# Sparse graph attention, one core: packed biases, planned constants, three more x buffers, norm constants by two tiles, and a new order of all work

## The chip, the cores and the metric

The kernel runs on one core of one Trainium2 chip. The metric is device time in microseconds (us) of one execution. Each number beside "time" is a median over runs; the profile comes from one execution.

## The reference, cut to what matters

x has 16 batches of 1024 rows with 512 columns; adj is one 1024 x 1024 matrix of zeros and ones, shared by all batches. Everything is float32.

```
h = jnp.maximum(_layernorm(x, axis=-1), 0.0)
q = (h @ Wq + bq).reshape(b, n, H, HD)        # H = 8, HD = 64; k and v likewise
scores = jnp.einsum('bihd,bjhd->bhij', q, k) / jnp.sqrt(jnp.float32(HD))
scores = scores + jnp.where(adj == 0, -1e9, 0.0)[None, None, :, :]
weights = jax.nn.softmax(scores, axis=-1)
out = jnp.einsum('bhij,bjhd->bihd', weights, v)
x = x + out.reshape(b, n, H * HD)
```

adj has few ones: most rows have a handful of neighbours, a few have many. So the kernel computes only the scores of neighbours.

## The kernel before, in words

**Once, at the start.** The kernel counts each row's neighbours (`degree`), ranks the rows by that count (`rank_of`, `ranks`), and from then on handles the rows in ranked order, in 8 tiles of 128 rows. Tile 0 has the rows with most neighbours. `CAPS` gives how many neighbour places each tile has (11, 8, 6, 5, 4, 3, 3, 2); what the rows of tile 0 have beyond is cut into pieces of 4 that get a pseudo tile, -1. The tables of neighbours are built by VectorE and scattered and collected through DRAM by DMAs (`list_of`, `spread`, `tell`, `collect`, `spots`); the chain `longest`, `count_pieces`, `first_piece`, `owners`, `pieces`, `slots` makes the places of the pieces. `first_piece` (line 794, `p_before`) is a matmul in it, and so stands in TensorE's queue.

**Each batch.** For each tile n: `load_x` (line 609, an indirect DMA from GpSimd's queue), `stats` on VectorE (L618, L619), then for a group of four tiles together `variance` on VectorE (L627), `power` on GpSimd (L630) and `shift` on VectorE (L634), then `norm` on ScalarE (L644), `flip` (four transposes on TensorE, L651), `unflip` (ScalarE copies to hT, L656), `proj_kv` (two projections on TensorE, one bias matmul L659 and four matmuls L661 each; each float32 matmul shows as two passes in the trace), `evict_kv` (ScalarE, L672), `store_kv` (an SP DMA into a key and value table in DRAM). When all 8 tiles of a batch are stored, rows of this table can be gathered. Batch 0's keys and values are made in a first pass over the rows in their given order (n = -8 to -1, names with `first`), while the ranks are still being found.

The attention goes by units. A unit is a tile with 2, 3 or 4 of its neighbour places; a batch has 14 units. For each: `queries` (a projection, L661 with `pq`), `gather` (GpSimd issues one indirect DMA of 512 KB for each place, L885; a row's own place comes by SP), `multiply` (VectorE, L895, which frees the query's PSUM buffer), `score` (L899), `exponent` (ScalarE, L903), for the tiles 4 to 7 `share`, then the weighing of v: one place on VectorE in some units (`weigh_v`, L915), the others on ScalarE (`weigh_s`, 8 activations a place, L921), `fold` (L926, on VectorE, or on GpSimd for the units in `POOL_FOLDS`) and `join` (L932) or `add_up` (TensorE, L944), `scale` (L976), `residual` (L985) and `put_out` (L988, an indirect DMA from GpSimd). An x tile is held from its load to its `put_out`.

**Buffers.** `POOLS` names how many buffers each pool has: 14 for x, 11 for hT, 2 for queries in PSUM, 2 for keys and values in PSUM, 2 for flips, 6 for gathered units.

**What sets the order.** Nothing is scheduled at run time. Each engine runs its own queue in order. The order is made when the program is built: `plan_of` (line 172) adds every operation to a `Plan` with its engine, a planned length and delay, what it follows, the buffers it uses, and a *place*, a number that ranks it. `Plan.ordered` (line 97) plays these through: whenever an engine is free in this planned time, it takes the ready operation with the lowest place. The list that results is the order in which the instructions are written. The last batch's units come in `LAST_ORDER`, tile 0 first.

**Biases.** Each bias is split into three bf16 parts that add up to it, in three rows of its own tile: `round` (ScalarE cast, L520), `remain` (GpSimd subtraction, L524), three times for each of k, v, q. The bias matmul uses `chosen`, which is one in these three rows:

```
def load_b(name):
    for start in starts:
        nc.sync.dma_start(rest[name][start : start + 1, :], vectors[name].rearrange("(o n) -> o n", o=1))
def round(name, j):
    rows = slice(starts[j], P)
    nc.scalar.copy(bias[name][rows, :], rest[name][rows, :])
```

Memsets and iotas for constants are issued at the very start of GpSimd's queue, ahead of all planned work.

**At the end.** `sums` (128 x 128 x 8) holds all row sums; `all_rows_fine` (line 1111) reduces it twice over 1024 elements (L1117, L1118), and a branch at the end reads the verdict.

Of the kernel before, what the change touches and what calls it, by code (L numbers as in the profile page):

```python
# [46 lines left out]
UNITS = (  # L47
    (7, 0, 2),
    (6, 0, 3),
    (5, 0, 3),  # L50
    (4, 0, 4),
    (3, 0, 3),
    (3, 3, 2),
    (2, 0, 3),
    (2, 3, 3),
    (1, 0, 4),
    (1, 4, 4),
    (0, 0, 4),
    (-1, 0, 4),
    (0, 4, 4),  # L60
    (0, 8, 3),
)
SHARES = (7, 6, 5, 4)
DIRECT = (7, 6, 5, 4, 3, 2, 1)
LAST_ORDER = (10, 11, 12, 13, 8, 9, 6, 7, 4, 5, 3, 2, 1, 0)
LAST_DIRECT = (7,)
POOL_FOLDS = (2, 3, 8, 9, 11)
# [5 lines left out]
ONE_MORE = (6,)  # L73
BY_VECTOR_LAST = {2: 1, 3: 1, 4: 1}
VECTOR_RESIDUAL = (4,)
POOLS = dict(x=14, h=2, pht=2, hT=11, pkv=2, kvt=3, q=2, q0=1, g=6, acc=2, o=1)


class Plan:
# [8 lines left out]
    def __init__(self):  # L88
        self.ops = []
        self.number = {}  # L90

    def add(self, key, engine, length, place, after=(), uses=(), delay=0.15, moves=0.0):

        self.number[key] = len(self.ops)
        self.ops.append((key, engine, length, place, after, uses, delay, moves))

    def ordered(self, bufs):
        ops = self.ops
# [29 lines left out]
        free = dict.fromkeys(engines, 0.0)  # L128
        moved = now = 0.0
        events = []  # L130
        result = []
        while True:
            for e in engines:
# [3 lines left out]
                while ready[e]:  # L137
                    place, i = heapq.heappop(ready[e])
                    key, _, length, _, _, uses, delay, moves = ops[i]
                    if can_start(ops[i]):  # L140
                        for use in uses:
                            if use not in has:
                                has.add(use)
                                given[use[0]] += 1
                        result.append(key)
                        free[e] = end = now + length
                        heapq.heappush(events, (end, -1))
                        if moves:
                            end = moved = max(moved, end) + moves
                        heapq.heappush(events, (end + delay, i))  # L150
                        break
# [16 lines left out]
        assert len(result) == len(ops)  # L168
        return result


def plan_of(B):

    plan = Plan()
    add = plan.add
    tiles, units, rate = B * NT, B * NU, NU / NT

    names = "kvq"
    sources = ("g", -3)
    first = range(-NT, 0)  # L180

# [4 lines left out]
    size = dict(load_x=0.75, load_w=3.0, load_adj=1.5, load_b=0.0)  # L186
    add(("zeros",), "SP", 0.15, -70, delay=2.0)
    for k, load in enumerate(loads):
        uses = [("x", load[1])] if load[0] == "load_x" else []
        add(load, "SP", 0.9 if load[0] == "load_b" else 0.2, -90 + k, uses=uses, delay=4.6, moves=size[load[0]])  # L190
    for j in range(3):
        for k, name in enumerate(names):
            place = -70 + 4 * k + j
            add(("round", name, j), "ACT", 0.58, place, [("remain", name, j - 1) if j else ("load_b", name)])
            if j < 2:
                add(("remain", name, j), "POOL", 1.3, place, [("round", name, j)])
    for t in range(NT):
        add(("degree", t), "DVE", 1.5, -60 + t, [("load_adj", t)])
        add(("no_diagonal", t), "POOL", 0.3, -60 + t, [("degree", t)])
    add(("keys",), "DVE", 0.4, -50, [("degree", t) for t in range(NT)], [sources])  # L200
    for what, known, made in (("key", [("keys",)], -48.59), ("rank", [("ranks",)], -37.92)):
        for half in range(2):
            row = ("q", what, half)
            add(("flip_row", what, half), "PE", 0.6, made, known, [row])
            add(("copy_row", what, half), ("DVE", "ACT")[half], 0.65, made, [("flip_row", what, half)], [row, sources])
    rows = lambda what: [("copy_row", what, half) for half in range(2)]
    for t in range(NT):
        add(("rank_of", t), ("DVE", "ACT")[t >= NT // 2], 1.25, (-53.17, -45.38)[t >= NT // 2], rows("key"))
    add(("ranks",), "DVE", 1.4, -47, [("rank_of", t) for t in range(NT)])
    add(("ends",), "DVE", 0.7, -45, rows("rank"), [sources])  # L210
    for t in range(NT):
        add(("list_of", t), "DVE", 2.5, -32.19 + t, [("ends",), ("no_diagonal", t)], [sources])
        behind = lambda name: [(name, t - 2)] if t > 1 else [("zeros",)]
        add(("tell", t), "POOL", 1.3, -38.67 + 0.3 * t, [("ranks",), ("shift", (t - NT) // 2)] + behind("tell"), delay=2.0)
        add(("spread", t), "POOL", 1.3, -45.82 + t, [("list_of", t)] + behind("spread"), delay=2.0)
    add(("collect", "told"), "SP", 0.05, -39, [("tell", t) for t in range(NT)], delay=2.6)
    add(("collect", "lists"), "SP", 0.05, -31, [("spread", t) for t in range(NT)], delay=2.6)
    add(("others",), "DVE", 1.3, -16.12, [("ends",)], [sources])
    add(("perm_of",), "DVE", 0.5, -31, [("collect", "told")])
    add(("spots",), "DVE", 3.9, -38.36, [("collect", "lists")])  # L220
    add(("long_rows",), "POOL", 1.3, -26.80, [("perm_of",)], [("g", -2)], 2.5, 1.5)
    add(("long_blocks", 0), "DVE", 1.25, -18.02, [("long_rows",), ("others",)], [sources, ("g", -2)])
    for k in range(1, 5):
        add(("long_blocks", k), "DVE", 2.0, -41.10 + 0.1 * k, [("long_blocks", k - 1)], [("g", -2)])
    for k in range(1, ROUNDS):
        known = [("long_blocks", 4), ("spots",)] if k == 1 else [("longest", k - 1)]
        add(("longest", k), "DVE", 1.1 if k == 1 else 0.8, --0.41 + 0.5 * k, known, [("g", -2)])
    a, own, lists = (("acc", "pieces", k) for k in range(3))
    add(("count_pieces",), "DVE", 0.9, 7.23, [("longest", ROUNDS - 1)])
    add(("first_piece",), "PE", 0.3, 2.20, [("count_pieces",)], [a])  # L230
    add(("owners",), "DVE", 0.9, 2.21, [("first_piece",)], [a])
    add(("flip_owners",), "PE", 0.3, 2.22, [("owners",)], [own])
    add(("copy_owners",), "DVE", 0.25, 2.23, [("flip_owners",)], [own])
    add(("list_pieces",), "PE", 0.4, 2.24, [("owners",)], [lists])
    add(("pieces",), "DVE", 1.1, 2.25, [("list_pieces",)], [lists])
    add(("slots", 0), "DVE", 2.0, 2.24, [("pieces",), ("spots",)])

    for n in range(-NT, tiles):
        b, j = divmod(n, NT)
        ahead = 0 if n >= 0 else 60 if n < 4 - NT else 19.47 - 1.3 * j  # L240
        p = (b - 1) * NU + j * rate if b > 0 else j * rate - 20.77 if b == 0 else 1.5 * j - 42.92
        if n >= 0:
            known = [("perm_of",)] if b == 0 else []
            add(("load_x", n), "POOL", 1.35, p - 5.47, known, [("x", n)], delay=4.5, moves=0.75)
        if b:
            add(("stats", n), "DVE", 0.84, p - ahead - 4.00, [("load_x", n)], [("x", n)])
        m, k, size = group_of(n)
        if b and k == size - 1:
            add(("variance", m), "DVE", 0.33, p - ahead - 5.38, [("stats", n - k) for k in range(size)])
            add(("power", m), "POOL", 1.1, p - ahead - 4.87, [("variance", m)])  # L250
            add(("shift", m), "DVE", 0.37, p - ahead - 4.29, [("power", m)])
        add(("norm", n), "ACT", 0.76, p - 6.38, [("shift", m) if b else ("load_x", n)], [("x", n), ("h", n)], delay=0.00)
        add(("flip", n), "PE", 0.62, p - 3.43, [("norm", n)], [("h", n), ("pht", n)])
        add(("unflip", n), "ACT", 0.53, p - 2.57, [("flip", n)], [("pht", n), ("hT", n)])
        if b == 0:
            continue
        for w in range(2):
            e = p - -0.51 + 0.3 * w + (1.41 if n < 3 - NT and w else 0.0)
            ready = [("unflip", n)]
            if n < 0:  # L260
                ready += [("round", "kv"[w], 2), ("load_w", "kv"[w])]
            add(("proj_kv", n, w), "PE", 3.70, e, ready, [("hT", n), ("pkv", n, w)])
            add(("evict_kv", n, w), "ACT", 0.53, e - 0.99, [("proj_kv", n, w)], [("pkv", n, w), ("kvt", n)])
        ready = [("evict_kv", n, w) for w in range(2)]
        if n >= 0:
            add(("store_kv", n), "SP", 0.1, p, ready, [("kvt", n)], delay=2.5, moves=1.5)
        else:
            add(("store_kv", n), "POOL", 1.35, p, ready + [("ranks",)] + ([("store_kv", n - 1)] if n > -NT else []), [("kvt", n)], delay=2.5, moves=1.5)

    q_of = {}  # L270
    one_by_one = []
    for k in range(units):
# [3 lines left out]
        i = b * NU + (LAST_ORDER.index(u) if b == B - 1 else u)  # L276
        t, _, count = UNITS[u]
        n = b * NT + NT - 1 - t
        q = ("q", b, t)
        if q not in q_of:  # L280
            p = i - 2.12
            if t >= 0:
                ready = [("unflip", n)] + ([("round", "q", 2), ("load_w", "q")] if b == 0 else [])
                add(("queries", b, t), "PE", 3.66, p, ready, [("hT", n), q])
                if t == 0:
                    add(("copy_q", b), "ACT", 0.57, p + 0.5, [("queries", b, 0)], [q, ("q0", b)])
            else:
                add(("queries", b, t), "PE", 0.9, p, [("copy_q", b)], [q, ("q0", b)])
# [4 lines left out]
        for s, slot in enumerate(slots):  # L293
            if is_own(u, s):
                add(slot, "SP", 0.1, i - -0.48, stored if b == 0 else [("store_kv", n)], [g], delay=2.5, moves=1.5)
                continue
            add(slot, "POOL", 1.35, i - 1.86 + 0.1 * s, stored, [g], delay=4.0, moves=1.5)
        vector = by_vector(b, B, u)
        add(("multiply", k), "DVE", 0.1 + 0.533 * count, i, slots + [q_of[q]], [g, q])
        add(("score", k), "DVE", 0.1 + 0.533 * count, i - -0.03, [("multiply", k)], [g])  # L300
# [887 lines left out]
```

## Time and profile before

| what | value |
|---|---|
| time, three runs | 1720.81 us median (1717.02 to 1721.78) |
| span of the profiled execution | 1721.4 us; the page gives no other time for this execution |
| instructions | 19566 |
| eight passes of one projection at full clock (L661 x8) | 3.60 us |
| bytes moved by DMA | 531.73 MB, 309 GB/s on average |
| TensorE busy in a stretch of 40 us, eight stretches from 320 us on | 36.5 to 40.0 us |

In the profile a line gives the source line, engine, operation, output and inputs. In a timeline the first number is the start, the second the length, and brackets show how long the engine had been idle and what ended the wait. "issue" is time in which the engine waited for nothing that the profile shows.

### The profile page before, as it was taken

How to read it: one execution, taken by the hardware profiler on the slowest of the kernel's cores; microseconds unless marked ns; L12 is line 12 of the kernel's file. 1: busy time of each engine (PE TensorE's matmuls, PEld its weight loads, DVE VectorE, ACT ScalarE, POOL GpSimd, SP SyncE). 2: the span in 40 equal slices, each digit the busy share in tenths (PEclk: the TensorE clock that was granted, in tenths of full speed). 3: DMA queues.
4: the chain of work that ended last, by engine and by line, in shares of the span. 5: the costliest groups of instructions: out<-in, count | busy, mean ns of one | idle time of the engine just before them, and what ended most of it. 6: DMA issues, size and time to landing. Idle time of an engine off the chain costs nothing.

```text
span 1721.4 us, 19566 instructions
## 1 busy us (share of the span) xinstructions
PE 1601.7 (93%) x4295; PEld 740.1 (43%) x4295; DVE 1506.2 (87%) x1921; ACT 1479.7 (86%) x5484; POOL 1264.2 (73%) x1161
## 2 busy tenths in 40 slices
PE   6979999999999999999999999999999999999896
PEld 3434444444444444444444444444444444444332
DVE  6789889898989989899998889989888998988896
ACT  5249989898998989899898989989898997979895
POOL 4757777787877778777877778778687777867654
PEclk9989999999999999999999999999999999999998
DMA  6397889899898989989898898889989888988893
GB/s 235 122 319 269 313 309 348 315 336 331 305 327 303 360 309 331 325 306 326 306 358 320 308 338 301 324 311 338 337 317 329 298 318 312 336 329 290 299 356 141
DMA packets 150741, 531.73 MB, mean 309 GB/s; under 512 B 19916, under 2 KB 19916, under 8 KB 150616
## 3 DMA queue, kind: packets, MB, share of 16 engines
q0 software_dynamic: 109840, 390.70, 64.4%
q1 hardware_dynamic: 40776, 139.71, 21.4%
q8 instruction: 36, 0.59, 0.1%
q14 instruction: 89, 0.73, 0.1%
HBM read 429.51 MB, written 100.82 MB: 308 GB/s over the span
## 4 chain that ended last, share of the span: by engine, by line
PE 74%; DMA 9%; DVE 3%; POOL 2%; ACT 1%; issue 1%; DVEq 0%; POOLq 0%; ACTq 0%
PE pv L661 22%; PE pk L661 22%; PE pq L661 20%; DMA g<-kv,index 8%; PE acc L944 3%; DVE g L895 2%; PE pht L651 2%; PE pv L659 1%; PE pk L659 1%; PE pq L659 1%; POOL g L885 1%; DMA kv<-kvt 1%; ACT hT L656 0%; ACT h L644 0%; DMA out_dram<-x,perm 0%
## 5 line engine op out<-in xcount | busy, mean ns | idle before, releaser
L921 ACT ACTIVATE g<-g,weights 128x64 f32<-128x64 f32 x4696 | 1155.8, 338 | 15.1 <-DVE weights L908 14.3
L885 POOL DMA_INDIRECT g<-kv,index x608 | 631.3, 1038 | 225.7 <-issue 144.5
L895 DVE TENSOR_TENSOR g<-g,pq 128x1536 f32<-128x1536 f32 (+2 forms) x208 | 388.1, 1871 | 101.6 <-DMA g<-kv,index 73.7
L661 PE MATMUL pq<-wq,hT 128*128 128x512 f32 x1024 | 470.8, 603 | 0.0
L661 PE MATMUL pk<-wk,hT 128*128 128x512 f32 x960 | 431.5, 592 | 0.0
L661 PE MATMUL pv<-wv,hT 128*128 128x512 f32 x960 | 431.5, 592 | 0.0
L899 DVE TENSOR_REDUCE weights<-g 128x32 f32<-128x2048 f32 (+2 forms) x224 | 424.1, 1893 | 0.6
L661 PEld LDWEIGHTS pq<-wq,hT 128*128 128x128 f32 x1024 | 198.1, 193 | 273.9 <-issue 270.1
L926 DVE TENSOR_TENSOR g<-g 128x512 f32<-128x512 f32 (+1 forms) x301 | 257.7, 860 | 27.6 <-ACT g L921 27.2
L661 PEld LDWEIGHTS pv<-wv,hT 128*128 128x128 f32 x960 | 182.4, 190 | 215.1 <-issue 212.0
L661 PEld LDWEIGHTS pk<-wk,hT 128*128 128x128 f32 x960 | 182.4, 190 | 205.5 <-issue 202.0
L609 POOL DMA_INDIRECT x<-in_x_dram,perm x128 | 148.8, 1162 | 39.9 <-issue 33.6
L988 POOL DMA_INDIRECT out_dram<-x,perm x128 | 133.7, 1045 | 50.9 <-issue 19.9
L926 POOL TENSOR_TENSOR g<-g 128x512 f32<-128x512 f32 x90 | 118.9, 1321 | 67.5 <-DVE g L926 58.6
L915 DVE TENSOR_TENSOR g<-g,weights 128x512 f32<-128x512 f32 x149 | 124.3, 834 | 2.1 <-ACT weights L903 1.8
L644 ACT ACTIVATE h<-x,shift,rstd 128x512 f32<-128x512 f32 x120 | 94.5, 812 | 28.7 <-issue 14.7
L903 ACT ACTIVATE weights<-weights 128x32 f32<-128x32 f32 (+2 forms) x224 | 49.7, 222 | 71.9 <-DVE weights L899 71.8
L985 POOL TENSOR_TENSOR x<-x,o 128x512 f32<-128x512 f32 x67 | 89.3, 1333 | 11.5 <-DVE o L976 7.8
L944 PE MATMUL acc<-g,ident 128*128 128x512 f32 x170 | 86.4, 622 | 9.0 <-DMA g<-kv,index 5.4
L659 PE MATMUL pq<-bq_parts,chosen 128*128 128x512 bf16 x128 | 48.8, 382 | 47.9 <-DVE g L895 47.9
L651 PE MATMUL pht<-ident,h 128*128 128x128 f32 x512 | 73.8, 276 | 18.5 <-ACT hT L656 16.5
L651 PEld LDWEIGHTS pht<-ident,h 128*128 128x128 f32 x512 | 60.6, 142 | 64.7 <-issue 33.9
(231 smaller groups left out, 1147.5 us busy)
## 6 DMA issues: line engine op xcount, KB each, us to landing
g<-kv SPq DMA_DIRECT2D x128, 512.0 KB
kv<-kvt SPq DMA_DIRECT2D x120, 512.0 KB
g<-kv,index POOLq DMA_INDIRECT x608, 6.8
adj<-in_adj_dram SPq DMA_DIRECT2D x8, 512.0 KB
x_first<-in_x_dram SPq DMA_DIRECT2D x8, 256.0 KB
x<-in_x_dram,perm POOLq DMA_INDIRECT x128, 6.3
out_dram<-x,perm POOLq DMA_INDIRECT x128, 5.5
wk<-in_L_gnn_Wk_dram SPq DMA_DIRECT2D x1, 1024.0 KB
```

The source lines that it names most:

```text
L609: nc.gpsimd.indirect_dma_start(out=X[n][:], out_offset=None, in_=x_rows, in_offset=on(ap=perm[:, t : t + 1], axis=0), element_offset=b * N * D
L651: nc.tensor.transpose(PH[n][:, c, :], hn[:, ts(c, P)], ident)
L659: nc.tensor.matmul(pt, chosen, bias[name], start=True, stop=False)
L661: nc.tensor.matmul(pt, HT[n][:, c, :], W[name][:, c, :], start=False, stop=(c == DC - 1))
L885: nc.gpsimd.indirect_dma_start(out=G[i][:, s].rearrange("p j d -> p (j d)"), out_offset=None, in_=KV[b % len(KV)][:], in_offset=on(ap=inde ...
L895: nc.vector.tensor_tensor(k, k, Q[b, t][:, None, :].to_broadcast([P, count, D]), ALU.mult)
L899: nc.vector.tensor_reduce(weights[:, w, :], heads(G[i][:, :count, 0, :]), AX.X, ALU.add)
L915: nc.vector.tensor_tensor(v, v, own.to_broadcast([P, n, H, HD]), ALU.mult)
L921: nc.scalar.activation(v[:, h, :], v[:, h, :], AF.Identity, scale=weights[:, c + s, h : h + 1])
L926: engine.tensor_tensor(v[:, 0:n], v[:, 0:n], v[:, first : first + n], ALU.add)
L944: nc.tensor.matmul(ACC[b, home], owner_t if t < 0 else ident, v[:, s, :], start=(u == parts_of(home)[0] and s == 0), stop=(u == parts_of(h ...
L988: nc.gpsimd.indirect_dma_start(out=out_rows, out_offset=on(ap=perm[:, t : t + 1], axis=0), in_=X.pop(b * NT + NT - 1 - t)[:], in_offset=No ...
```

## The change

- The three biases share one tile: three copies of k's bias go to partitions 0 to 2, of v's to 32 to 34, of q's to 64 to 66, each by one DMA. `round` and `remain` handle all at once; which row keeps which part is set by a scale per partition (`parts_at` makes it from the identity). `chosen` has one block for each bias. The very first tile (n = -8) is projected without its bias, which a matmul of its own (`add_bias`) adds afterwards.
- Constants become planned operations (`setup`, three steps on GpSimd); two memsets move to VectorE; an activation on a constant, `warm`, stands first on ScalarE.
- x has 17 buffers instead of 14.
- `variance`, `power`, `shift` handle two tiles at a time instead of four.
- Row sums are kept for each batch; a new operation `seen` reduces them to a sum and a minimum per batch; the last check reduces 16 numbers of each.
- The plan's lengths and delays are new (`LENGTHS`, `PAIR`). The plan lets VectorE and GpSimd not run two operations of `SHARED` at the same planned time. All places are new (`AT`, and `FINE` for single operations), and the place of a unit grows by its share of the batch's slots instead of by one.
- `JOIN` is False, so `join_acc` is not used. `LAST_TILES` and `PARTS` give the units and their order as before; the units folded on GpSimd are the same.

Shortened diff:

```diff
-POOLS = dict(x=14, h=2, pht=2, hT=11, pkv=2, kvt=3, q=2, q0=1, g=6, acc=2, o=1)
+AT = dict(
+    load_x=106.07, stats=-2.83, variance=-3.87, power=-87.25, shift=-9.66, norm=-4.89, flip=-7.74, unflip=-31.23, proj_kv=-1.94,
+    evict_kv=38.12, queries=-1.19, own=55.32, gather=-1.08, score=6.6, exponent=29.51, row_sums=-147.93, share=2.3,
+    weigh_v=-2.68, weigh_s=90.78, fold=-2.21, join=-4.72, add_up=-1.79, direct_residual=35.08, direct_out=32.8, more=-13.17,
...
+POOLS = dict(x=17, h=2, pht=2, hT=11, pkv=2, kvt=3, q=2, q0=1, g=6, acc=2, o=1)
+GROUP = 2
+JOIN = False
...
+SHARED = ("fold", "join",  "weigh_v", "residual", "scale", "power")
...
+                    shared = e in port and key[0] in SHARED
+                    if can_start(ops[i]) and not (shared and port[other[e]] > now):
+                        if shared:
+                            port[e] = now + length
...
-            add(slot, "POOL", 1.35, i - 1.86 + 0.1 * s, stored, [g], delay=4.0, moves=1.5)
+            add(slot, "POOL", i + AT["gather"] + 0.1 * s, stored, [g])
...
-            add(("fold", k, *n), "POOL" if on_pool else "DVE", 1.4 if on_pool else 0.45 * n[1] + 0.35, i + 0.90, weighed, [g], delay=1.67 if on_pool else 0.15)
+            add(("fold", k, *n_), "POOL" if on_pool else "DVE", i + AT["fold"], weighed, [g], length=None if on_pool else PAIR[n_[1]])
...
-    size = 4 if n >= 0 else 2
+    size = GROUP if n >= 0 else 2
...
         def load_b(name):
-            for start in starts:
-                nc.sync.dma_start(rest[name][start : start + 1, :], vectors[name].rearrange("(o n) -> o n", o=1))
+            vec = vectors[name]
+            rows = bass.AP(tensor=vec.tensor, offset=vec.offset, ap=[[0, 3], [1, H * HD]])
+            g = names.index(name)
+            nc.sync.dma_start(rest[32 * g : 32 * g + 3, :], rows)
+
+        def warm():
+            nc.scalar.activation(warmed, minus_half, AF.Relu, bias=minus_half, scale=minus_half)
+
+        def parts_at():
+
+            ends_at = [once.tile([P, 1], F32, tag=f"ends{j}", name=f"ends_at_{j}") for j in range(2)]
+            for j in range(2):
+                nc.vector.tensor_reduce(ends_at[j], ident.rearrange("p (g r) -> p g r", r=32)[:, :, j], AX.X, ALU.add)
+            nc.vector.tensor_scalar(later[0], ends_at[0], -1.0, 1.0, op0=ALU.mult, op1=ALU.add)
+            nc.vector.tensor_tensor(later[1], later[0], ends_at[1], ALU.subtract)
+
+        def round(j):
+
+            if j < 2:
+                nc.scalar.activation(part, rest, AF.Identity, scale=later[j])
+            else:
+                nc.scalar.copy(bias, rest)
+
+        def remain(j):
+            nc.gpsimd.tensor_tensor(rest, rest, part, ALU.subtract)
...
+        def setup(k):
+
+            count_up = lambda to, base, step, by: nc.gpsimd.iota(
+                to, pattern=[[step, to.shape[-1]]], base=base, channel_multiplier=by, allow_small_or_imprecise_dtypes=True
+            )
+            if k == 0:
+                nc.gpsimd.memset(chosen, 0.0)
+                for g in range(len(names)):
+                    nc.gpsimd.memset(chosen[32 * g : 32 * g + 32, g, :], 1.0)
+            elif k == 1:
+                count_up(place, 0, P, 1)
+                nc.gpsimd.memset(before["lists"], 0.0)
+                nc.gpsimd.tensor_copy(before["told"][:, :, own], place)
+                count_up(limits, P, P, 0)
+            else:
+                count_up(small_iota, 0, 1, 0)
+                nc.gpsimd.memset(spot, 0.0)
+                nc.gpsimd.memset(weights, 0.0)
...
+        def add_bias(n, name):
+            pt = PT[n, names.index(name)]
+            nc.tensor.matmul(pt, chosen[:, names.index(name), :], bias, start=False, stop=True)
...
+        def seen(b):
+            nc.vector.tensor_reduce(sums[:, 0, b : b + 1], SUMS[b].rearrange("p t h -> p (t h)"), AX.X, ALU.add)
+            nc.vector.tensor_reduce(sums[:, 1, b : b + 1], SUMS.pop(b).rearrange("p t h -> p (t h)"), AX.X, ALU.min)
...
-    nc.vector.tensor_reduce(both[:, 0:1], flat, AX.X, ALU.add)
-    nc.vector.tensor_reduce(both[:, 1:2], flat, AX.X, ALU.min)
+    nc.vector.tensor_reduce(both[:, 0:1], sums[:, 0, :], AX.X, ALU.add)
+    nc.vector.tensor_reduce(both[:, 1:2], sums[:, 1, :], AX.X, ALU.min)
```

## The prediction, made before the changed kernel ran

> **What bounds the kernel now.** I read the page's busy table first, then a table of busy time by stage (start, first batch, the middle up to the last key and value projection, the rest), then TensorE's own rows in order of time, then the rows of the constants for the norm.
>
> ```profile
> PE 1601.7 (93%) x4295; PEld 740.1 (43%) x4295; DVE 1506.2 (87%) x1921; ACT 1479.7 (86%) x5484; POOL 1264.2 (73%) x1161
> ```
>
> ```profile
> 0.00:31.00 31.00, 13.87 (x44) 7.79 (x45) 18.28 (x51) 13.82 (x22) 16.80 (x37) 0.97 0.74 267
> 31.00:200.00 169.00, 155.69 (x442) 74.39 (x441) 145.85 (x290) 108.51 (x345) 113.78 (x105) 0.96 0.71 246
> 200.00:1616.00 1416.00, 1353.51 (x3636) 625.02 (x3635) 1262.09 (x1495) 1280.38 (x4799) 1074.41 (x962) 0.99 0.89 321
> 1616.00:1721.40 105.40, 78.66 (x176) 32.90 (x174) 79.93 (x88) 76.98 (x321) 59.21 (x57) 0.86 0.69 257
> ```
>
> Columns: stretch and length, then busy us of TensorE, its weight loads, VectorE, ScalarE and GpSimd, granted clock, DMA share, GB/s. TensorE's idle time is 17.1, 13.3, 62.4 and 26.7 us; it bounds the first three stages. The other engines and the DMAs are near it: in the middle VectorE is busy 89%, ScalarE 90%, DMA 89%.
>
> The middle is fourteen repeats of about 100.7 us (boundaries at 207, 308, ... 1618). One boundary, TensorE only:
>
> ```profile
> 307.88 1.02 PE L944 MATMUL acc<-g,owner_t 128*128 128x512 f32 x2
> 308.74 1.02 PE L944 MATMUL acc<-g,ident 128*128 128x512 f32 x2
> 311.64 0.38 PE L659 MATMUL pq<-bq_parts,chosen 128*128 128x512 bf16 x1 [1.88 <-DVE g L895]
> 311.86 3.59 PE L661 MATMUL pq<-wq,hT 128*128 128x512 f32 x8
> 315.29 1.02 PE L944 MATMUL acc<-g,ident 128*128 128x512 f32 x2
> 316.14 1.04 PE L651 MATMUL pht<-ident,h 128*128 128x128 f32 x8
> 318.44 0.38 PE L659 MATMUL pq<-bq_parts,chosen 128*128 128x512 bf16 x1 [1.26 <-DVE g L895]
> ```
>
> TensorE stops twice for a query buffer: the multiply that frees it waits for a gather, which waits for the last tile of the batch to be stored. No next-batch projection is at hand in between, for this reason:
>
> ```profile
> 305.08 0.64 DVE L618 BATCH_NORM_STATS2 st<-x 128x6 f32<-128x512 f32 x1
> 307.39 0.16 DVE L627 TENSOR_SCALAR rstd<-mv 128x4 f32<-128x4 f32 x1
> 312.04 1.53 POOL L630 TENSOR_TENSOR rstd<-rstd,minus_half 128x4 f32<-128x4 f32 x1
> 314.31 0.15 DVE L634 SCALAR_TENSOR_TENSOR shift<-mv,rstd 128x4 f32<-128x4 f32 x1
> 314.50 1.52 ACT L644 ACTIVATE h<-x,shift,rstd 128x512 f32<-128x512 f32 x2 [0.46 <-DVE shift L634]
> ```
>
> The constants wait until four tiles are loaded and measured, and the power then stands behind gathers on GpSimd. Loads of x at 293.84 wait for output of older tiles (1.86 us instead of 0.95). So the first new norm comes at 314.5, too late for the gap.
>
> The start and the end:
>
> ```profile
> 9.46 1.28 ACT L520 ACT_TABLE_LOAD   x1 [9.46 <-DMA scratch<-in_L_gnn_bk_dram]
> 11.51 1.15 POOL L524 TENSOR_TENSOR scratch<-scratch,bk_parts 64x512 f32<-64x512 f32 x1 [4.42 <-ACT bk_parts L520]
> 12.74 0.73 POOL L630 TENSOR_TENSOR before_told<-before_told,minus_half 128x2 f32<-128x2 f32 x1
> ...
> 1704.65 1.17 DVE L1117 TENSOR_REDUCE c_both<-sums 128x1 f32<-128x1024 f32 x1
> 1705.82 1.21 DVE L1118 TENSOR_REDUCE c_both<-sums 128x1 f32<-128x1024 f32 x1
> 1706.95 0.68 DVE L915 TENSOR_TENSOR g<-g,weights 128x512 f32<-128x512 f32 x1
> ```
>
> The first power, ready at 5.9, stands behind a bias subtraction that waits for a table load, which waits for a bias DMA. At the end two long reduces stand ahead of the last weighing.
>
> **The change, part by part, against the span of 1721.4 us.**
>
> Biases and the first operations. Nine casts (0.615 us, 5.5 on ScalarE) become three; six subtractions (1.155 us, 6.9 on GpSimd) two; nine 2 KB DMAs, which hold SP's queue from 2.6 to 10.2, three. Added are some four small VectorE operations (about 0.8 us, taking the 0.2 us of small rows). The power need no longer pass the bias chain: about 6.2 to 6.9, norm to 7.8, flip and copy to 9.2. The weights' landing is not shown: 1.5 MB at this stage's 267 GB/s plus the 3.1 us from the first load's issue (0.81) to its first use (3.92) gives about 9.5. So projections can begin at 9.5 instead of 17.25. Afterwards wv arrives behind 7 MB: about 29 us at that rate, as now (first pv at 29.79), so only the two further key projections of 3.65 us fit in earlier. I take idle time from 17.1 to 11: -6 (bounds -1 and -8).
>
> The index chain. TensorE's queue stands 8.40 us (to 105.1) behind p_before, placed too early in the order; VectorE makes its input at 104.8. With measured lengths in the plan work can be put ahead of it: -6 (bounds 0 and -8; if VectorE's chain were moved back for it, nothing).
>
> Middle. Constants by two and three more x buffers let two tiles be normed before the gap: one tile's pair of projections is 7.3 us, against gaps of 1.9 and 1.3. The fourteen boundaries hold 47.5 us of waiting for VectorE; a third flip in a row waits for ScalarE, 0.99 us fourteen times, and pairs of tiles avoid it. The other 1.0 are single waits. Of the 62.4 I leave 1.2 us per batch, 17: -45 (bounds: 0, if no tile is ready in time, to -60). After the gap the next limits are the gathers and VectorE: 89.8 us per batch against a new period near 97.
>
> The clock. After gaps of 1.37, 2.27, 4.11 and 3.74 us the eight passes behind them took 5.29, 5.29, 6.01 and 5.29 us instead of 3.60: 7.5 us together. The Trainium skill (TensorE: Matmul & The Clock Gate, HAM oscillation) asks only that idle gaps stay below about 3.4 us; by it the first two should be free and the gain at most 4.1. Here the row decides[...]. -5.
>
> Added work. Sixty powers instead of thirty: a two-column one took 0.714 us, a four-column one 1.206, so 42.8 instead of 36.2. Thirty more variances and shifts (0.16 each) are 9.5 us of VectorE; thirty-two reduces over 64 elements (0.25, between the rows of 48 and 72) are 8. Together 1.2 us of VectorE per batch, inside its 10.9 us of idle. One rule speaks against this: the Trainium skill (SBUF — State Buffer, SBUF: two separate sides) says that GpSimd and a two-input VectorE operation lock each other out for a whole instruction. The trace agrees: the 0.68 us weighing took up to 2.2 and 0.83 on average. By the rule each added power may hold VectorE for its length: 6.6 us more in all; if none meets, 0. The plan keeps them apart in planned time only. By the row nearest to it, weighing, some 0.15 of 0.68 is lost, 1.5 us. With the new fills of the queues at 94% I charge 4 (bounds -2, since moved folds may meet less, and +20).
>
> End. Two reduces (2.38) ahead of the last weighing become two short ones (0.3) and the last batch's share of the new ones (0.5): -1.6. The 63 us of additions and queries on TensorE from 1640 to 1703 stay. The gap between the last store and the first new multiply (1616 to 1630) stays, but may take more work: -2 (bounds +4, -8). Sum -3.5.
>
> The constants planned as GpSimd operations cost nothing while no load of adj has landed (16 us); were that cover gone, some 3 us.
>
> Sum: -6 - 6 - 45 - 5 + 4 - 3.5 = -61.5; 1721.4 - 61.5 = 1660. The profile gives no other time for its execution; its span lies 0.6 above the median of 1720.81, so I keep 1660.
>
> **Rivals.**
>
> The cover does not come. For it: eleven hT buffers stay, eight of them full at a boundary; loads of x now have the last place on GpSimd (+106), so the buffers may fill late; VectorE, ScalarE and DMA at 89 to 90% leave room for only ten percent. Against: DMA reached 360 GB/s in one slice, and loads wait for x buffers now. Then the middle stays, and start, index chain and end give 15.5, less the added 4, plus perhaps a third of the middle's 50: 1721 - 28 = 1693.
>
> The gap moves to GpSimd. The new places put folds (-2.2) and powers (-87) ahead of gathers (-1.1), where folds stood behind them (+0.9 against -1.9). GpSimd runs in order: a fold that waits for VectorE holds the gathers behind it, and these hold the multiply, the query buffer and TensorE. Now 23 such waits in the middle cost 48.8 us, 3.8 at most, mostly covered. If one of 3.8 and a power of 1.05 stand ahead of the first gathers of each of fourteen batches and the cover is used up, that adds 68 us to a kernel with start and end gains of 15.5 and added work of 4: 1778; with only half of the boundaries hit, 1744. It decides from 0.8 us per batch if the middle gains nothing, from 4.4 if it gains 50. Against it: GpSimd has 24 us idle per batch.
>
> The change does not do what it says: places that fit the planned clock, not the chip, move gaps about and gains cancel: 1720.
>
> **How the numbers follow.** The likeliest case 0.57 (1640 to 1685), the missing cover 0.23 (1680 to 1712), moved gap 0.15 (1727 to 1780), cancelling 0.05. Within 0.3% is about what a measurement of this kernel can tell from no change. Faster 0.80, same 0.05, slower 0.15. The range runs from 1636 to 1712: it leaves out the slower cases and little below.
>
> **What would show it.** First projection near 10 instead of 17.25; no wait near 8 us at p_before; boundaries with a key projection between the two queries and gaps below 1 us; TensorE idle in the middle under 25 us and a period near 97.5; no group of eight passes above 4 us there; VectorE's idle at gathers (75 us) lower. I am wrong if the period stays near 100, if gathers wait behind folds, or if weighing grows well over 0.83 us.

## The result and the profile after

| what | before | after |
|---|---|---|
| time, median of four runs each | 1721.30 us (1717.02 to 1724.56) | 1672.13 us (1669.52 to 1674.53) |
| span of the profiled execution | 1721.4 us | 1667.8 us |
| time of that execution | not given | 1669.52 us |

The ratio after to before is 0.9702, with a 95% interval of 0.9672 to 0.9732: faster by 49 us. The forecast was 1660, with a range of 1636 to 1712.

First the busy table of the changed kernel (busy us, share of the span, instructions), then its busy time by stage. The columns are those of the same table in the prediction; the third stage ends here where the last key and value projection does, at 1554 us.

```profile
PE 1593.1 (96%) x4295; PEld 736.8 (44%) x4295; DVE 1482.5 (89%) x2019; ACT 1470.0 (88%) x5479; POOL 1271.2 (76%) x1184
```

```profile
0.00:31.00 31.00, 16.80 (x54) 9.09 (x55) 21.42 (x63) 13.99 (x22) 9.55 (x31) 1.00 0.86 305
31.00:200.00 169.00, 164.25 (x480) 79.10 (x479) 145.91 (x309) 116.69 (x372) 121.62 (x115) 0.99 0.73 257
200.00:1554.00 1354.00, 1332.47 (x3589) 614.52 (x3588) 1225.90 (x1548) 1253.30 (x4731) 1075.89 (x979) 1.00 0.93 332
1554.00:1667.80 113.80, 79.61 (x177) 34.11 (x175) 89.24 (x102) 86.05 (x358) 64.12 (x61) 0.83 0.72 257
```

TensorE's idle time, length less busy, gives the balance. The span shrank by 53.6 us:

| term | before | after | measured | forecast |
|---|---|---|---|---|
| start, idle | 17.1 | 14.2 | -2.9 | -6 |
| index chain (first batch), idle | 13.3 | 4.75 | -8.6 | -6 |
| middle, idle | 62.4 | 21.5 | -40.9 | -45 |
| end, idle | 26.7 | 34.2 | +7.5 | -3.5 |
| TensorE busy | 1601.7 | 1593.1 | -8.6 | -5 (clock) |
| added work | | | inside the rows above | +4 |

The middle carries the gain: from one `p_more` to the next lie 97.7 us there in the median, 101.0 before. One boundary of the changed kernel, TensorE's rows in order:

```profile
582.98 0.38 PE L797 MATMUL pq<-bias_parts,chosen 128*128 128x512 bf16 x1
583.19 3.60 PE L799 MATMUL pq<-wq,hT 128*128 128x512 f32 x8
587.77 1.13 PE L1084 MATMUL acc<-g,ident 128*128 128x512 f32 x2 [0.98 <-DVE g L1062]
...
589.09 3.59 PE L799 MATMUL pq<-wq,hT 128*128 128x512 f32 x8
592.52 0.38 PE L797 MATMUL pk<-bias_parts,chosen 128*128 128x512 bf16 x1
592.74 3.60 PE L799 MATMUL pk<-wk,hT 128*128 128x512 f32 x8
596.17 1.02 PE L1084 MATMUL acc<-g,owner_t 128*128 128x512 f32 x2
597.03 1.25 PE L786 MATMUL pht<-ident,h 128*128 128x128 f32 x8
598.12 0.38 PE L797 MATMUL pv<-bias_parts,chosen 128*128 128x512 bf16 x1
598.33 3.60 PE L799 MATMUL pv<-wv,hT 128*128 128x512 f32 x8
```

Where TensorE stood twice for a query buffer, a key and a value projection of the next batch (592.74 and 598.33) now follow the query of 589.09. What is left is one gap of 0.98 for a fold. The side that waits has changed as well. VectorE's waits before, then after (engine, line, releaser: us in total, times, longest):

```profile
DVE g L895 <- DMA g<-kv,index: 75.4, 46, 4.4
...
DVE g L895 <- PE pq L661: 10.5, 11, 2.5
```

```profile
DVE g L1031 <- PE pq L799: 64.5, 21, 5.2
DVE x L1134 <- POOL g L1062: 31.2, 14, 2.5
DVE g L1068 <- POOL g L1062: 14.9, 12, 1.2
...
DVE g L1031 <- DMA g<-kv,index: 12.4, 9, 3.8
```

The multiply used to wait for gathers; now it waits for the query that TensorE makes. TensorE, busy 96% of the middle before, is busy 98% of it now.

### The profile page after: what moved, and what is told of

Read it like the earlier page. It is cut to its first block, busy times and chain, and to the rows that moved or that the text cites. A ratio compares the mean times of both kernels' runs of the same rounds, so it can differ in the third digit from the quotient of the medians.

```text
span 1667.8 us, 19582 instructions
## 1 busy us (share of the span) xinstructions
PE 1593.1 (96%) x4295; PEld 736.8 (44%) x4295; DVE 1482.5 (89%) x2019; ACT 1470.0 (88%) x5479; POOL 1271.2 (76%) x1184
## 3 DMA queue, kind: packets, MB, share of 16 engines
q1 hardware_dynamic: 40776, 139.71, 22.9%
## 5 line engine op out<-in xcount | busy, mean ns | idle before, releaser
L1021 POOL DMA_INDIRECT g<-kv,index x608 | 637.8, 1049 | 247.5 <-issue 166.2
L799 PE MATMUL pq<-wq,hT 128*128 128x512 f32 x1024 | 460.4, 593 | 0.0
L1035 DVE TENSOR_REDUCE weights<-g 128x24 f32<-128x1536 f32 (+2 forms) x224 | 420.9, 1895 | 0.5
L1137 POOL DMA_INDIRECT out_dram<-x,perm x128 | 148.6, 1161 | 36.8 <-issue 24.9
L744 POOL DMA_INDIRECT x<-in_x_dram,perm x128 | 140.9, 1100 | 35.2 <-issue 34.9
L1039 ACT ACTIVATE weights<-weights 128x24 f32<-128x24 f32 (+2 forms) x224 | 49.0, 219 | 100.8 <-DVE weights L1035 99.7
L1051 DVE TENSOR_TENSOR g<-g,weights 128x512 f32<-128x512 f32 x149 | 104.2, 700 | 0.6
L753 DVE BATCH_NORM_STATS2 st<-x 128x6 f32<-128x512 f32 x120 | 81.9, 682 | 3.6 <-DMA x<-in_x_dram,perm 3.6
L814 ACT COPY kvt<-pk 128x512 f32<-128x512 f32 x120 | 68.7, 572 | 9.7 <-PE pk L799 9.7
```

What stands on the lines that cost most here:

```text
L744: nc.gpsimd.indirect_dma_start(out=X[n][:], out_offset=None, in_=x_rows, in_offset=on(ap=perm[:, t : t + 1], axis=0), element_offset=b * N * D
L799: nc.tensor.matmul(pt, HT[n][:, c, :], W[name][:, c, :], start=(apart and c == 0), stop=(not apart and c == DC - 1))
L1021: nc.gpsimd.indirect_dma_start(out=G[i][:, s].rearrange("p j d -> p (j d)"), out_offset=None, in_=KV[b % len(KV)][:], in_offset=on(ap=inde ...
L1035: nc.vector.tensor_reduce(weights[:, w, :], heads(G[i][:, :count, 0, :]), AX.X, ALU.add)
L1051: nc.vector.tensor_tensor(v, v, own.to_broadcast([P, n, H, HD]), ALU.mult)
L1137: nc.gpsimd.indirect_dma_start(out=out_rows, out_offset=on(ap=perm[:, t : t + 1], axis=0), in_=X.pop(b * NT + TILES.index(t))[:], in_offse ...
```

## The experiments

Three explanations were to be told apart. In the first (A where an expectation uses the letter), buffers and pairs of tiles put a normed tile into the gap, and that is the gain. In the second (C), the gain comes from places fitted to measured lengths, whatever the buffers. In the third, the rule for VectorE and GpSimd carries it. Where an expectation has a B, it says itself what B is. Each ratio is to the kernel before, run again beside the experiment: 1722.37 us for e1 to e4, 1729.76 for e5 to e8, 1723.97 for e9 to e12. Across these groups, compare the ratios and not the microseconds.

### One constant of the change put back, places kept

e1 puts back the buffers, e2 the groups of four, e3 both:

```diff
-POOLS = dict(x=17, ...)
+POOLS = dict(x=14, ...)     # e1, e3
-GROUP = 2
+GROUP = 4                   # e2, e3
```

> The changed kernel with 14 buffers for x instead of 17; its order is found again by the same planner with the same places. Theory A (the cover at the batch boundary comes from x tiles loaded early enough): the loads wait for buffers again, TensorE waits for VectorE at query buffers at the boundaries again, about 2 to 3 us for each of 14 batches: 1700 to 1715. Theory B (the new places and lengths do it, buffers hardly matter): within 5 us of 1672.

> The changed kernel with the constants for the norm made by four tiles again, 17 buffers for x. Theory A (pairs are needed to have a tile ready in the gap): gaps come back in part, 1685 to 1700. Theory B (order alone): 1668 to 1677; it saves 30 small operations on GpSimd and 60 on VectorE, worth at most some us. With 17 buffers four tiles may be loaded early enough anyway, which would also give the latter.

> The changed kernel with 14 buffers and constants by four tiles: what is left is the new plan, the packed biases and the short check. Theory A: most of the middle's gain of 41 us of idle time goes, 1705 to 1720. Theory B: 1670 to 1680.

Measured: 1921.08 (ratio 1.1151, 1.1130 to 1.1173), 1866.34 (1.0845, 1.0815 to 1.0874) and 1988.04 (1.1536, 1.1514 to 1.1558), against 1722.37 before. All three are far slower than the kernel before, which has 14 buffers and groups of four, and far outside what either theory expected. TensorE's waits in e1:

```profile
PE pht L786 <- ACT h L779: 64.9, 16, 22.9
PE acc L1084 <- issue: 58.3, 6, 15.7
PE pq L797 <- DVE g L1031: 50.1, 13, 6.8
```

A flip waits up to 22.9 us for a normed tile, and all that TensorE has queued behind it waits too. The plan makes another order from the same places when it has fewer buffers, and that order is bad. So the three runs show that the places are bound to their setting. They don't give the price of a buffer or of a pair.

### Buffers and pairs on the kernel before, in its own order

```diff
-POOLS = dict(x=14, ...)
+POOLS = dict(x=16, ...)
-    size = 4 if n >= 0 else 2
+    size = 2
-    sums = keep.tile([P, B * NT, H], F32, ...)
+    sums = keep.tile([P, 2 * NT, H], F32, ...)
-            s = sums[:, b * NT + t, :]
+            s = sums[:, b % 2 * NT + t, :]
```

> The kernel before with 16 buffers for x and constants by two tiles, old places and lengths. To make room, the table of row sums holds two batches only, so the last check sees only the last two batches' sums; that leaves out part of the check. Theory A: some of the middle's gain comes already here, 1680 to 1705. Theory B: the old order keeps its gaps, 1715 to 1725.

Measured: 1719.35, ratio 0.9988 (0.9970 to 1.0007): no difference, in B's range. TensorE's longest wait in it, and VectorE's wait for gathers:

```profile
PE acc L944 <- issue: 36.9, 8, 8.0
```

```profile
DVE g L895 <- DMA g<-kv,index: 36.1, 30, 4.1
```

The queries' waits (47.5 us in the middle of before) are no longer among TensorE's longest and VectorE's wait for gathers halves (75.4 to 36.1), but other waits take their place, such as the additions' 36.9 us. The buffers and pairs were there, and this order did not turn them into time. The first explanation alone falls, for 16 buffers; 17 in this order were not run.

### The change with the places of the kernel before

```diff
-AT = dict(load_x=106.07, stats=-2.83, variance=-3.87, power=-87.25, ...)
-FINE = {...}
+AT = dict(load_x=-5.47, stats=-4.0, variance=-5.38, power=-4.87, ...)
+FINE = {}
```

> The changed kernel (17 buffers, pairs, measured lengths, packed biases, short check) with the places of the kernel before and no corrections for single operations. Theory A (buffers and pairs give the cover, given lengths that fit): near the changed kernel, 1672 to 1690. Theory C (the places found for this setting carry the gain): 1700 to 1725. The first run with old places, 16 buffers and pairs under the old lengths gave no gain, which speaks for C.

Measured: 1746.39, ratio 1.0135 (1.0098 to 1.0172): slower than before, by a little over one per cent, and above both ranges. VectorE's first wait in it:

```profile
DVE g L1013 <- DMA g<-kv,index: 82.4, 49, 4.8
```

It is the wait of before (75.4). So three more buffers, pairs, packed biases, new lengths and the rule for the two engines give nothing with these places: the change needs its new ones. It is not the order of the kernel before, though. The places are the same offsets, but the units' base still grows by their share of the slots, and the lengths are the new ones.

### Places searched for each setting

e10 has 14 buffers and pairs, e11 17 and groups of four, e12 14 and groups of four; the places in `AT` are found anew for each. In e10 `FINE` is empty; e11 and e12 keep the corrections that were made for the change. The rest is as in the change:

```diff
-POOLS = dict(x=17, ...)
+POOLS = dict(x=14, ...)     # e10, e12
-GROUP = 2
+GROUP = 4                   # e11, e12
-AT = dict(load_x=106.07, ...)
+AT = dict(...)              # its own in each
-FINE = {...}
+FINE = {}                   # e10 only
```

> The changed kernel with 14 buffers for x, and places found anew for that setting, without corrections for single operations (a search over the places, as the change's own places were found for 17). The run with 14 buffers and the places for 17 was slow because the plan no longer fitted. Theory A (three more buffers are needed for the cover): 1695 to 1715, TensorE waiting at the boundaries. Theory C (the order does it): 1675 to 1695.

> The changed kernel with constants by four tiles, 17 buffers, and places found anew for that setting. Theory A (pairs are needed in the gap): 1690 to 1705. Theory C, or cover by the buffers alone: 1670 to 1690.

> The changed kernel with 14 buffers and constants by four tiles, and places found anew for that setting: the plan, the packed biases and the short check alone. Theory A (buffers and pairs carry the middle's 41 us): 1705 to 1725, gaps at the boundaries as before. Theory C (order carries it): 1685 to 1705.

| x buffers | groups of four | pairs |
|---|---|---|
| 14 | 1773.20, ratio 1.0273 (1.0232 to 1.0315) | 1715.48, ratio 0.9964 (0.9932 to 0.9996) |
| 17 | 1701.49, ratio 0.9862 (0.9825 to 0.9898) | the change: 1672.13, ratio 0.9702 |

TensorE's longest waits in e10, then in e12:

```profile
PE pht_first L768 <- ACT h_first L761: 14.9, 2, 13.5
PE pht L768 <- ACT h L761: 13.9, 18, 2.5
```

```profile
PE pht L779 <- ACT h L772: 45.0, 27, 3.8
PE p_more L1097 <- DVE more L1093: 20.4, 2, 10.6
```

e11 lies in A's range, e10 just above it, e12 above both of its ranges. With the old buffers and groups a flip waits 45.0 us for a norm, with pairs 13.9, with 17 buffers (e11) 2.7. Between these orders, pairs at 14 buffers are worth 58 us (1773.20 - 1715.48) and buffers at groups of four 72 us (1773.20 - 1701.49). From e10 and e11 on to the change the ratio falls by 0.026 and 0.016, some 45 and 28 us.

None of these is the price of a buffer or a pair. The 58 us also hold the different `FINE`. e12 has the buffers and groups of the kernel before and is slower than it, so a better order for its setting exists. How long each search was is not on record, and one order for each setting doesn't tell how far another search would come. The runs suggest that pairs and buffers help when the order is fitted to them; they don't show it. That the second explanation could do without both is not excluded either.

### The rule that keeps VectorE and GpSimd apart

```diff
-SHARED = ("fold", "join",  "weigh_v", "residual", "scale", "power")
+SHARED = ()
```

> The changed kernel whose plan lets VectorE and GpSimd run port-sharing operations at the same planned time (the list of such operations is empty). Theory A (keeping them apart in the plan keeps them apart on the chip): the mean weighing on VectorE goes from 0.70 us back towards 0.83, VectorE loses some 2 us a batch, and since TensorE bounds the middle by a few per cent only, 1675 to 1690. Theory B (it does not matter, because TensorE is the bound): within 4 us of 1672.

Measured: 1791.05, ratio 1.0363 (1.0319 to 1.0406), above both ranges. The group for the weighing, in before, after and e5 (times, busy us, mean ns, idle before it and its releaser):

```profile
L915 DVE TENSOR_TENSOR g<-g,weights 128x512 f32<-128x512 f32 x149 | 124.3, 834 | 2.1 <-ACT weights L903 1.8
```

```profile
L1051 DVE TENSOR_TENSOR g<-g,weights 128x512 f32<-128x512 f32 x149 | 104.2, 700 | 0.6
```

```profile
L1051 DVE TENSOR_TENSOR g<-g,weights 128x512 f32<-128x512 f32 x149 | 119.5, 802 | 0.8 <-ACT weights L1039 0.4
```

834 ns before, 700 with the rule, 802 without. Each weighing can be set beside GpSimd's operations with two inputs in the trace. Of the 149, 51 run at the same time as one of these in before, 16 with the rule, 34 without. Those that meet none take 0.67 us on average in all three kernels; those that do take 1.15, 0.93 and 1.23. So keeping the operations apart in planned time keeps most of them apart on the chip. VectorE is busy 1482.5 us with the rule and 1529.2 without. The 1791 itself can't be put down to this. The places were fitted to a plan with the rule, and flips wait 56.1 us for norms in e5, as in e1.

### The start: the first power ahead of the biases

```diff
-            add(("remain", j), "POOL", AT["parts"] + j, [("round", j)])
+            add(("remain", j), "POOL", AT["parts"] + j, [("round", j), ("power", -NT // 2)])
```

> The changed kernel with one more dependency in the plan: the first subtraction of the bias parts follows the first power, so that GpSimd's queue has the power ahead. Expected from the trace: the power ran at 11.81 behind a subtraction that waited until 10.70 for the bias; its input was ready at 5.5. The first norm comes near 7 instead of 12.8 and the first projection near 9.5 instead of 15.4, if the weights have landed. Theory A (the start is a term of the sum): 3 to 6 us faster than the changed kernel, 1666 to 1669. Theory B (the value weights and the index chain, bounded by DMA, set what follows): no difference, 1672.

Measured: 1674.32, ratio 0.9681 (0.9640 to 0.9722), inside the change's interval. The start of the changed kernel, then of e6:

```profile
9.89 0.72 ACT L654 ACTIVATE scratch<-scratch,later 128x512 bf16<-128x512 f32 x1 [7.40 <-DMA scratch<-in_L_gnn_bq_dram]
10.70 1.15 POOL L659 TENSOR_TENSOR scratch<-scratch 128x512 f32<-128x512 f32 x1 [6.93 <-ACT scratch L654]
11.81 0.72 POOL L765 TENSOR_TENSOR before_told<-before_told,minus_half 128x2 f32<-128x2 f32 x1
...
15.41 4.83 PE L799 MATMUL pk_first<-wk,hT_first 128*128 128x512 f32 x8
...
26.48 1.88 PE L799 MATMUL pv_first<-wv,hT_first 128*128 128x512 f32 x4
```

```profile
5.62 0.72 POOL L765 TENSOR_TENSOR before_told<-before_told,minus_half 128x2 f32<-128x2 f32 x1 [1.84 <-DVE before_told L762]
8.70 0.72 ACT L654 ACTIVATE scratch<-scratch,later 128x512 bf16<-128x512 f32 x1 [6.20 <-DMA scratch<-in_L_gnn_bq_dram]
9.32 1.51 ACT L779 ACTIVATE h_first<-x_first,before_told 128x512 f32<-128x512 f32 x2
...
11.97 4.63 PE L799 MATMUL pk_first<-wk,hT_first 128*128 128x512 f32 x8
...
24.27 1.97 PE L691 MATMUL p_key<-ident,key 128*128 128x128 f32 x8 [2.94 <-DVE key L680]
26.04 2.20 PE L799 MATMUL pv_first<-wv,hT_first 128*128 128x512 f32 x3
```

In the changed kernel the power (11.81) still stands behind the first bias subtraction. In e6 it runs at 5.62 and the first projection starts 3.44 us earlier, but TensorE then waits 2.94 us at `p_key`, and the first value projection moves only from 26.48 to 26.04. The norm (9.32) still stands behind a bias cast, now on ScalarE (8.70), so it does not come near 7 as expected. TensorE is busy 17.9 of the first 31 us instead of 16.8: the start gives about 1 us this way.

### The end: where the last batch's work stands

e7 takes the additions of two more of the last batch's tiles (6 and 5) from TensorE and folds their places on VectorE and GpSimd; e8 moves `p_more` of the last batch behind the first unit's additions:

```diff
-LAST_DIRECT = (7,)
+LAST_DIRECT = (7, 6, 5)                      # e7
-    place_of(pieces[0]) + AT["pass_on"]
+    place_of(pieces[0]) + (AT["pass_on"] if b < B - 1 else 5.0)   # e8
```

> The changed kernel with the last batch's tiles 6 and 5 treated like those of the other batches: places folded on VectorE and GpSimd instead of added up by TensorE. TensorE is busy without a gap for 66 us near the end, VectorE 81% of that. It loses six places of additions of 0.86 us. Theory A (TensorE bounds the last 66 us): 3 to 5 us faster. Theory B (VectorE or ScalarE would be late at once, tail is balanced): no gain, or 2 to 5 us slower.

> The changed kernel with the last batch's small matmul p_more placed behind the additions of the first unit. TensorE waits 7.49 us at it at 1581.8 to 1589.3 while the first unit's additions could start at about 1584. Theory A (order at this one spot): 3.4 us of additions move into the wait, 3 to 5 us faster. Theory B (the waiting is for ScalarE's weighing of the first unit and for gathers): within 1 us.

Measured: e7 1679.13, ratio 0.9702 (0.9663 to 0.9740): no gain, as B has it. e8 1670.06, ratio 0.9650 (0.9610 to 0.9689): the lowest, though its interval meets the change's. TensorE's gaps after the last key and value projection, in the changed kernel and in e8:

```profile
1566.24 2.05 PE L1084 MATMUL acc<-g,ident 128*128 128x512 f32 x2 [8.49 <-issue]
...
1579.77 2.05 PE L1084 MATMUL acc<-g,ident 128*128 128x512 f32 x2 [2.92 <-issue]
1589.31 0.60 PE L1104 MATMUL p_more<-more,owner_t 128*128 128x8 f32 x2 [7.49 <-DVE more L1100]
1589.76 6.12 PE L1084 MATMUL acc<-g,ident 128*128 128x512 f32 x8
```

```profile
1574.06 2.05 PE L1084 MATMUL acc<-g,ident 128*128 128x512 f32 x2 [9.94 <-issue]
...
1586.58 6.61 PE L1084 MATMUL acc<-g,ident 128*128 128x512 f32 x10 [2.92 <-issue]
1596.47 0.36 PE L1104 MATMUL p_more<-more,owner_t 128*128 128x8 f32 x2 [3.27 <-DVE more L1100]
```

In e8 eight additions that stood behind `p_more` run ahead of it (the row of ten begins with two that did so before), and its wait falls from 7.49 to 3.27. Whether the time falls with it by a few us is not settled. In e7 and e8 the plan is made anew, and the last key and value projection ends 6 to 7 us later than in the change (1560.9 and 1560.3 instead of 1553.9), so neither run changes the end alone. No version here is clearly better than the change.

## Why the prediction was right, and where it missed

**Mechanism.** The boundary shows what the forecast rested on: a next-batch key projection right behind a query, a largest gap of 0.98 there, a period of 97.7 (forecast near 97.5), 21.5 us of idle time in the middle (forecast 17; under 25). -40.9 against -45 leaves 1.5 us per batch instead of the 1.2 that I took. What the forecast did not separate is what makes this happen. It charged the middle to buffers and pairs. The runs show that 16 buffers and pairs are worth nothing in the old order (0.9988), that the change with the old places loses (1.0135), and that the change's own places lose without pairs (1.0845) or without the buffers (1.1151). So the gain belongs to the places and the settings together; whether a better order could do without the settings is not shown.

**The sum** was helped by errors that cancel. Start, middle and end gave 18.2 us less than forecast; the index chain, TensorE's busy time and the added work, which did not show, came out 10.2 us better. That 61.5 forecast and 53.6 measured lie so near each other is in part luck.

**The end is the mis-sized term:** -3.5 forecast, +7.5 measured. The step that failed is "The gap between the last store and the first new multiply (1616 to 1630) stays, but may take more work: -2 (bounds +4, -8)". The gap grew. From the last key and value projection to the stretch in which TensorE is busy without a break, before had 29.5 us with 11.4 idle; the changed kernel has 35 us with 22.0 idle, 10.7 more. The last key and value projection ends 62 us earlier (1615.8 to 1553.9), which is more than the whole gain. But VectorE was then busy with units of the batch before (30.4 of the 35 us, ScalarE 30.8), and its first multiply of the last batch came at 1572.78, 18.9 us behind that projection instead of 14.3. TensorE ran ahead in the middle, and part of the lead was given back where it has only the last batch to work on. What its longest wait there (8.49) was for, the profile doesn't show.

The unbroken stretch did not stay at 63 us: TensorE is busy 66.4 of 67 us up to 1656. The other part of the term went better than forecast. From TensorE's last addition to the end of the span lie 12.1 us instead of 15.2, against -1.6 forecast. The two last reduces took 0.16 and 0.15, and those of a batch 0.21 each (0.25 taken).

**The start:** -6 forecast, -2.9 measured; the first projection came at 15.41 and not near 10. The assumption "the power need no longer pass the bias chain" was wrong: the dependency was gone, the order was not. The bias DMAs were issued at 2.2 to 3.0 and the first cast that needs them ran at 9.89, so the subtraction held GpSimd and the power behind it. e6 shows that with the power ahead only about 1 us comes back: the norm still stands behind a cast, and then VectorE's `key` of the index chain is not ready. So the second assumption, that two more key projections fit in, was wrong as well.

**The index chain** gave -8.6, at the far bound of what I took (0 to -8). The wait of 8.40 at `p_before` is gone; one of 3.46 for a norm has come at 94.94. The matmul before, then after:

```profile
105.11 0.59 PE L794 MATMUL p_before<-has,owner_t 128*128 128x1 f32 x2 [8.40 <-DVE owner_t L791]
```

```profile
106.45 0.28 PE L934 MATMUL p_before<-has,owner_t 128*128 128x1 f32 x2
```

**The clock:** -5 forecast. Five groups of eight passes in the middle of before took 5.29 to 6.01 us, 9.2 us more than 3.60 each; in the middle of the changed kernel none took over 3.7. TensorE's busy time fell by 8.6, which is of that size; the slower end (clock 0.83 instead of 0.86) takes a little. It would be natural to suppose that short gaps cost where they lie close together. Two places of before speak against that:

```profile
218.27 0.38 PE L659 MATMUL pq<-bq_parts,chosen 128*128 128x512 bf16 x1 [2.12 <-DVE g L895]
218.49 3.59 PE L661 MATMUL pq<-wq,hT 128*128 128x512 f32 x8
...
1118.00 0.42 PE L659 MATMUL pq<-bq_parts,chosen 128*128 128x512 bf16 x1 [2.06 <-DVE g L895]
1118.22 5.29 PE L661 MATMUL pq<-wq,hT 128*128 128x512 f32 x8
```

The gap of 2.12 came 7.7 us behind one of 1.97, and the passes behind both kept 3.59; the gap of 2.06 stood alone, and the passes behind it took 5.29. So short gaps cost in some places, as the charge of 5 assumes, but neither their length nor their nearness tells where.

**Added work** was charged with 4 us and did not show. VectorE's busy time fell by 23.7 us with 98 more instructions. The sixty powers took 45.3 us, near the forecast 42.8. The Trainium skill (SBUF — State Buffer, SBUF: two separate sides) says that a GpSimd operation and a VectorE operation with two inputs lock each other out; I took from it a cost of more powers. The trace agrees that meeting costs time: 0.67 us for the weighings that meet no such operation, 0.93 to 1.23 for those that do. That one blocks the other outright, no run here shows. But fewer met: from before to after the weighing lost 20 us (149 x 0.134), and from e5 to the change, where the rule is all that was edited, 15 us.

**Rivals.** The cover came, so 1693 did not. Folds on GpSimd did not hold the gathers: the multiply's wait for gathers fell from 75.4 to 12.4. The rival in which places fit the plan and not the chip is refuted for the change, but close to what e1 to e3 and e5 show: places that fit another plan made the kernel 61 to 266 us slower than before.

**What stays open:** how the gain divides between buffers, pairs, lengths and places, and whether the old buffers and groups could reach it too, which only an equal search for each setting would tell; how much of e5's loss comes from such meetings; and whether e8 beats the change.

## What to carry to other kernels

In an order made at build time, a part of a change that was fitted together can't be priced by putting that part back. Here 16 buffers and pairs together were worth nothing in one order, and putting back the groups or the buffers cost some 195 or 250 us in another. Fit the order anew for each setting that you compare, and give each the same search. And when the bounding engine gains in the repeated part, look at the tail. Here TensorE's idle time there grew by 7.5 us, while the other engines still held work of the batch before; count the last batch's first wait as a possible cost of running ahead.

## What the runs showed of the hardware that was not expected

- The DMA engines were busy 93% at 332 GB/s over 1354 us (89% and 321 before), and the gathers' median time from issue to landing stayed at 6.8 us in both.
- The last of three 6 KB bias loads, issued at 2.96 us, ended the wait of the first cast only at 9.89 in the changed kernel and 8.70 in e6: 5.7 to 6.9 us. The 1 MB weight load issued just ahead of them took 7.5 us.
- In the middle of the changed kernel, at a granted clock of 1.00, even the one gap of 2.08 us (at 306.0) was followed by eight passes in 3.60 us. In before a single gap of 2.06 us was followed by 5.29.
